# A two-layer graph kernel: statistics of a weight part on ScalarE, and node tiles transposed by DMA

## The chip, the cores and the metric

The kernel runs on one core of a Trainium2 chip. The metric is the device time of one execution in microseconds, the median of several runs. Before the change it is 2240.1 us (three runs, 2240.02 to 2240.91).

## The reference

Two layers work on 3327 nodes with 1024 features each. The first normalises the nodes, quantises them to 4 bits, multiplies them with a quantised 1024 x 1024 weight and sums over the neighbours; the second is graph attention with 8 heads and a small dense network behind it. The change lies in the first product, so only this part matters here:

```python
h = jnp.maximum(_layernorm(x, axis=-1), 0.0)
mean = jnp.mean(weight)
std = jnp.std(weight, ddof=1)
weight_q = _weight_quant((weight - mean) / std, wgt_alpha, 3)
xq = _act_quant(h, act_alpha, 4)
support = jnp.matmul(xq / act_delta, weight_q / wgt_delta) * act_delta * wgt_delta
support_q = _act_quant(jax.nn.relu(support), act_alpha2, 4)
output = jnp.matmul(adj / adj_scaling_factor, support_q / support_delta)
```

The mean and the deviation of the weight go over the whole matrix, so nothing of it can be rounded before all of it has been read.

## The kernel before

The nodes are padded to 26 tiles of 128 rows (T = 26), and the features make 8 blocks of 128 (KF = 8). The work runs in stages: the first computes the quantised support of every tile, `s_int`; the second multiplies it with the adjacency, split into a high and a low part (lines 170 to 179 and 680), and prepares the attention; a third does the attention and a last one the dense layers. This text is about the first stage, lines 194 to 569.

**The weight.** SP issues the two halves of node tile 0, then the eight parts of w, each 128 x 1024 numbers, and then the node tiles 1 to 5. The statistics of a part are made in one of two ways. On VectorE they are two BN_STATS of 512 columns (line 364). On ScalarE (`measure_on_scalar`, lines 248 to 258) they are a pass that sums the part, two small scalings, and a second pass that sums the squares of the deviations; each pass is an ACTIVATE and a read of the accumulator. Parts 0 and 3 go to ScalarE (`BY_ACT`, line 352), the other six to VectorE. One BN_AGGR (line 410) joins all of it, two tiny matmuls with a constant matrix (lines 412 and 419) join the partitions, and then the weight is rounded and clamped in 16 pieces, on ScalarE, VectorE and GpSimd.

**A node tile** goes through these steps. The names in brackets are those of the written order.

- Its rows are loaded on SP in pairs (`load_pair`, line 128), into three buffers of two tiles each. A pair is loaded when ScalarE has read the pair three before it.
- Two BN_STATS and a BN_AGGR on VectorE give mean and variance (stats, mv; lines 234 and 241).
- The norm of a pair of tiles (norm, lines 260 to 287) is a chain of eight tiny operations. Its square root is on ScalarE, the reciprocals are on VectorE, and the rest is on VectorE in the written order and on GpSimd in the loop.
- ScalarE normalises the tile, applies the relu and writes bytes (bytes, line 293). VectorE clips these to 15 and writes bf16 (clip, line 301).
- The tile is transposed into `xqt`, of which there are four buffers. Either a DMA transpose on SP does it, issued in the same step as the clip (line 305), or TensorE does it with eight matmuls into PSUM (turn, line 311) and a copy on ScalarE (turned, line 314). `by_tensor` (line 295) chooses: TensorE takes tiles 0, 1, 2, 3, 4, 6, 9, 12, 15, 18, 21 and 24.
- Sixteen matmuls of 512 columns make the product (product, line 321). ScalarE rescales the result and writes bytes (sum, line 336), and VectorE clips them into `s_int` (support, line 339).

**The order.** Every compute instruction of this stage is pinned to program order on its engine. Up to the product of tile 7 the order is written out by hand as a list of steps, `ORDER` (lines 479 to 509). From tile 8 on a loop makes it (lines 543 to 567): in round t it measures tile t + 6, makes the sum and the support of t - 1, the bytes and the clip of t + 3, and the product of t, between whose halves it transposes tile t + 2 where that is TensorE's. In even rounds it also issues the loads of tiles t + 8 and t + 9, ahead of the transpose of t + 3. SP's queue is in order as well. In round 24 the first adjacency load is issued there (line 170).

Of the kernel before, what the change touches and what calls it, by code (L numbers as in the profile page):

```python
# [8 lines left out]
F32 = mybir.dt.float32  # L9
# [11 lines left out]
P = 128  # L21
N = 3327
T = (N + P - 1) // P
# [3 lines left out]
KF = F // P  # L27
# [33 lines left out]
def two_layer_kernel(  # L61
# [101 lines left out]
    with tc.tile_pool(name="at", bufs=2, reuse_waits="tile") as atp:  # L163
# [35 lines left out]
        with tc.tile_pool(name="s1", bufs=2, reuse_waits="tile") as s1, tc.tile_pool(  # L199
            name="s1_mm", bufs=3, space=PSUM, reuse_waits="tile"  # L200
        ) as mm_ps, tc.tile_pool(name="s1_tp", bufs=2, space=PSUM, reuse_waits="tile") as tp_ps:
            w_int = s1.tile([P, KF, F], BF16, name="w_int", bufs=1)
            w_stats = s1.tile([P, 2 + 4 * (KF - 2), 3], F32, name="w_stats", bufs=1)

            def pin(ins):
                tc.keep_in_program_order(ins)
# [17 lines left out]
            def load_pair(t0):  # L224
                part = load(t0)
                for q in range(GT):
                    part(q)
# [15 lines left out]
            def measure(t):  # L243
                for c in range(FC):
                    half_stats(t, c)
                aggregate(t)

            def measure_on_scalar(mean, squares, src, name):

                junk = s1.tile([P, F], BF16, tag="xq", name="junk", bufs=3)  # L250
                total, nmean = (s1.tile([P, 1], F32, name=name + c, bufs=1) for c in "tm")
                pin(nc.scalar.activation(junk, src, AF.Copy, accum_out=total))
                pin(nc.scalar.activation(nmean, total, AF.Copy, scale=-1.0 / F))
                pin(nc.scalar.activation(mean, total, AF.Copy, scale=1.0 / F))
                yield
                junk = s1.tile([P, F], BF16, tag="xq", name="junk", bufs=3)
                pin(nc.scalar.activation(junk, src, AF.Square, bias=nmean, accum_out=squares))
                yield

            def normaliser(p, engine=nc.gpsimd):  # L260

                v, s, r, q, nb = (
                    small.tile([P, GT], F32, tag=f"l0{c}", name=f"l0{c}") for c in "vsrqb"
                )
                mv = mvs.pop(p)

                def own(ins):
                    if engine is nc.vector:
                        pin(ins)

                own(engine.tensor_scalar(v, mv[:, :, 1], EPS, None, ALU.add))
                yield
                pin(nc.scalar.activation(s, v, AF.Sqrt))
                yield
                pin(nc.vector.reciprocal(r, s))
                yield
                own(engine.tensor_tensor(q, v, r, ALU.mult))
                own(engine.tensor_tensor(q, q, s, ALU.add))
                yield
                pin(nc.vector.reciprocal(r, q))  # L280
                yield
                own(engine.tensor_scalar(r, r, to_q, -1.0, ALU.mult, ALU.mult))
                own(engine.tensor_tensor(nb, mv[:, :, 0], r, ALU.mult))
                own(engine.tensor_scalar(r, r, -1.0, None, ALU.mult))
                for i in range(GT):
                    ready[GT * p + i] = r[:, i : i + 1], nb[:, i : i + 1]
                yield


            def to_bytes(t):  # L290
                rs, nb = ready.pop(t)
                xbs[t] = s1.tile([P, F], U8, name="xb")
                pin(nc.scalar.activation(xbs[t], rows.pop(t), AF.Relu, bias=nb, scale=rs))

            def by_tensor(t):
                return t % 3 == 0 or t in (1, 2, 4)

            def quantise(t, engine=nc.vector):

                xq = xqs[t] = s1.tile([P, F], BF16, name="xq", bufs=3)  # L300
                pin(engine.tensor_scalar(xq, xbs.pop(t), QA, None, ALU.min))

                xqts[t] = s1.tile([P, KF, P], BF16, name="xqt", bufs=4)
                if not by_tensor(t):
                    nc.sync.dma_start_transpose(xqts[t], xqs.pop(t))

            def transpose(t):
                tps[t] = tp_ps.tile([P, KF, P], BF16, name="tp")
                xq = xqs.pop(t)
                for k in range(KF):  # L310
                    pin(nc.tensor.transpose(tps[t][:, k, :], xq[:, k * P : (k + 1) * P], ident_b))

            def transposed(t):
                pin(nc.scalar.copy(xqts[t], tps.pop(t)))
# [19 lines left out]
            def support_bytes(t):  # L334
                sbs[t] = s1.tile([P, F], U8, tag="sb", name="sb", bufs=3)
                pin(nc.scalar.activation(sbs[t], mms.pop(t), AF.Relu, scale=to_s))

            def support(t, engine=nc.vector):
                pin(engine.tensor_scalar(s_int[t], sbs.pop(t), QA, None, ALU.min))
# [9 lines left out]
                loads[q // GT](q % GT)  # L349


            BY_ACT = (0, 3)
            for i in range(len(BY_ACT)):
                nc.gpsimd.memset(w_stats[:, i, 0:1], float(F))
            by_act = [
                measure_on_scalar(w_stats[:, i, 1:2], w_stats[:, i, 2:3], w[:, k], f"w{k}")
                for i, k in enumerate(BY_ACT)
            ]

            def weight_statistics(k):  # L360
                at = len(BY_ACT) + 4 * (k - sum(k > b for b in BY_ACT))
                for c in range(FC):
                    d = w_stats[:, at + 2 * c : at + 2 * c + 2].rearrange("p n s -> p (n s)")
                    pin(nc.vector.bn_stats(d, w[:, k, c * 512 : (c + 1) * 512]))
# [34 lines left out]
            to_s = const.tile([P, 1], F32, name="to_s")  # L399
            nc.gpsimd.tensor_tensor(to_s, act_delta, wgt_delta, ALU.mult)  # L400
            nc.gpsimd.tensor_scalar(to_s, to_s, r_aa2, QA, ALU.mult, ALU.mult)
            for k in (2, 4, 5, 6, 7):
                weight_statistics(k)
                if k == 2:
                    for _ in range(2):
                        next(by_act[1])
                    transposed(0)

            w_mv = small.tile([P, 2], F32, name="w_mv")
            pin(nc.vector.bn_aggr(w_mv, w_stats.rearrange("p n s -> p (n s)")))  # L410
# [61 lines left out]
            def bytes_of(t):  # L472
# [27 lines left out]
                norm_4 product_5_0_5_7 norm_4 product_5_1_0_0 norm_4 product_5_1_1_1 turn_6 norm_4 norm_4  # L500
                product_5_1_2_2 turned_6 support_1 product_5_1_3_5 stats_10_0 product_5_1_6_6 bytes_8
                product_5_1_7_7 product_6_0_0_0 stats_11_0 product_6_0_1_3 support_2 product_6_0_4_4 sum_4
                product_6_0_5_7 clip_8 product_6_1_0_1 sum_5 product_6_1_2_2 stats_10_1 product_6_1_3_5
                stats_11_1 product_6_1_6_6 bytes_9 product_6_1_7_7 product_7_0_0_0 mv_10 product_7_0_1_1
                mv_11 product_7_0_2_2 norm_5 product_7_0_3_3 support_3 product_7_0_4_4 norm_5
                product_7_0_5_6 norm_5 sum_6 product_7_0_7_7 norm_5 product_7_1_0_1 norm_5 product_7_1_2_2
                norm_5 product_7_1_3_4 clip_9 bytes_10 product_7_1_5_7 support_4 turn_9 turned_9 clip_10
                stats_12_0 stats_13_0 stats_12_1 stats_13_1 mv_12 mv_13 support_5 support_6
            """.split()
            V = nc.vector  # L510
            supp = ExitStack()
# [31 lines left out]
            for t in range(8, T):  # L543
                if t == T - 2:
                    part = next(columns)
                pair = t // 2 + 2
                steps = iter(())
                if t % GT == 0 and pair < T // GT:
                    steps = normaliser(pair)
                for _ in range(4):  # L550
                    next(steps, None)
                if t + 6 < T:
                    measure(t + 6)
                for _ in steps:
                    pass
                support_bytes(t - 1)
                support(t - 1)
                if t + 3 < T:
                    to_bytes(t + 3)
                    if t % GT == 0 and t + 8 < T:  # L560
                        load_pair(t + 8)
                    quantise(t + 3)
                products(t, 0)
                if t + 2 < T and by_tensor(t + 2):
                    transpose(t + 2)
                    transposed(t + 2)
                products(t, 1)
            support_bytes(T - 1)
            support(T - 1)
# [2 lines left out]
        with tc.tile_pool(name="wh", bufs=1, reuse_waits="tile") as whp, tc.tile_pool(  # L572
            name="s2", bufs=2, reuse_waits="tile"
        ) as s2, tc.tile_pool(name="mm", bufs=2, space=PSUM, reuse_waits="tile") as mm_ps, tc.tile_pool(
            name="s2_wh", bufs=2, space=PSUM, reuse_waits="tile"
        ) as wh_ps, tc.tile_pool(name="s2_sp", bufs=1, space=PSUM, reuse_waits="tile") as sp_ps, tc.tile_pool(
            name="s2_last", bufs=1, space=PSUM, reuse_waits="tile"
# [90 lines left out]
            for t in range(T):  # L668
# [3 lines left out]
                for js in PARTS:  # L672
                    hi, lo = part
                    part = next(columns, None)
# [54 lines left out]
    with tc.tile_pool(name="mf0", bufs=1, reuse_waits="tile") as mf0, tc.tile_pool(  # L729
        name="srow0", bufs=1, reuse_waits="tile"  # L730
    ) as srow0, tc.tile_pool(name="sel", bufs=4, reuse_waits="tile") as selp, tc.tile_pool(
        name="srow1", bufs=1, reuse_waits="tile"
    ) as srow1, tc.tile_pool(name="mf1", bufs=1, reuse_waits="tile") as mf1, tc.tile_pool(
        name="md", bufs=2, reuse_waits="tile"
    ) as mdp, tc.tile_pool(name="f1", bufs=1, reuse_waits="tile") as f1p, tc.tile_pool(
        name="s3", bufs=1, reuse_waits="tile"
    ) as s3, tc.tile_pool(
        name="s3_acc", bufs=7, space=PSUM, reuse_waits="tile"
# [147 lines left out]
        for i, (c, g, e, si) in enumerate(attends):  # L886
# [82 lines left out]
            for j in range(T):  # L969
                n = i * T + j  # L970
                k, m = divmod(n - 20, 2 * T)
# [43 lines left out]
    with tc.tile_pool(name="s4", bufs=2, reuse_waits="tile") as s4, tc.tile_pool(  # L1015
        name="s4_ps", bufs=4, space=PSUM, reuse_waits="tile"
# [103 lines left out]
```

## Time and profile before

| | |
|---|---|
| median of three runs | 2240.1 us |
| the profiled execution, its time | 2241.67 us |
| its span, first to last instruction | 2239.9 us |
| TensorE busy in the span | 2190.0 us |
| first weight product of a tile (line 321) | 24.74 us |
| first matmul of the second stage (line 680) | 128.41 us |
| mean granted clock of TensorE | 0.998 |

The profiled execution is one execution of the program, and all times in it count from its first instruction. A row of the timeline gives start, length, engine, line and operation, and, in brackets, how long the engine was idle before it and what ended the wait. Rows of the same kind that follow each other are merged. [...] The landing of a DMA is counted from its issue.

### The profile page before, as it was taken

How to read it: one execution, taken by the hardware profiler on the slowest of the kernel's cores; microseconds unless marked ns; L12 is line 12 of the kernel's file. 1: busy time of each engine (PE TensorE's matmuls, PEld its weight loads, DVE VectorE, ACT ScalarE, POOL GpSimd, SP SyncE). 2: the span in 40 equal slices, each digit the busy share in tenths (PEclk: the TensorE clock that was granted, in tenths of full speed). 3: DMA queues.
4: the chain of work that ended last, by engine and by line, in shares of the span. 5: the costliest groups of instructions: out<-in, count | busy, mean ns of one | idle time of the engine just before them, and what ended most of it. 6: DMA issues, size and time to landing. Idle time of an engine off the chain costs nothing.

```text
span 2239.9 us, 31268 instructions
## 1 busy us (share of the span) xinstructions
PE 2190.0 (98%) x12470; PEld 1747.2 (78%) x12480; DVE 1536.8 (69%) x1996; ACT 1114.9 (50%) x1685; POOL 180.4 (8%) x269
## 2 busy tenths in 40 slices
PE   5999999999999999899999999999999999999998
PEld 2477777766677777699999999999999999744444
DVE  8745555554455545588999999999999999822211
ACT  6734444444454444357566556565555655531120
POOL 2301101110111101000000000000000000000000
PEclk9999999999999999999999999999999999999999
DMA  6665566555665556934242341654242432383311
GB/s 216 161 196 158 157 182 183 170 168 146 183 181 171 162 158 189 310 128 148 83 139 88 93 131 33 225 175 151 86 148 83 138 89 77 100 208 104 113 56 56
DMA packets 241203, 321.68 MB, mean 144 GB/s; under 512 B 104021, under 2 KB 184869, under 8 KB 241057
## 3 DMA queue, kind: packets, MB, share of 16 engines
q1 hardware_dynamic: 220504, 246.50, 36.8%
q0 software_dynamic: 20544, 73.18, 10.4%
q8 instruction: 98, 1.61, 0.3%
q14 instruction: 49, 0.39, 0.1%
q10 hardware_dynamic: 8, 0.00, 0.0%
HBM read 209.25 MB, written 86.79 MB: 132 GB/s over the span
## 4 chain that ended last, share of the span: by engine, by line
PE 53%; ACT 1%; DVE 0%; DMA 0%; issue 0%; DVEq 0%
PE acc L993 27%; PE mps L786 13%; PE o L1064 8%; PE h_ps L1027 4%; ACT enct L1049 0%; PE h_ps L949 0%; DMA weights<-in_w1t 0%; ACT h L1034 0%; DVE sel L984 0%; DVE nodes L1060 0%; ACT su L830 0%; DVE su L827 0%; DVE yo L1074 0%; ACT rest L957 0%; DVEq L1117 0%
## 5 line engine op out<-in xcount | busy, mean ns | idle before, releaser
L984 DVE SCALAR_TENSOR_TENSOR sel<-srow,ndst,mask 128x896 fp32r<-128x896 f32 (+1 forms) x832 | 864.8, 1081 | 52.3 <-PE acc L993 47.2
L786 PE MATMUL mps<-dw,mf 128*128 128x260 f32 x2704 | 452.4, 283 | 0.1
L680 PE MATMUL mm<-s_int,hi 128*128 128x512 f32 x1352 | 427.2, 397 | 0.0
L680 PE MATMUL mm<-s_int,lo 128*128 128x512 f32 x1352 | 419.1, 391 | 0.0
L993 PE MATMUL acc<-f_even,sel 128*128 128x260 f32 x2704 | 399.6, 285 | 6.7 <-issue 5.0
L993 PE MATMUL acc<-f_odd,sel 128*128 128x260 f32 x2704 | 393.8, 286 | 1.0 <-ACT xs L1008 1.0
L785 ACT CAST mf<-mask 128x1664 fp32r<-128x1664 uint8 x208 | 331.4, 1594 | 113.0 <-PE mps L786 94.9
L786 PEld LDWEIGHTS mps<-dw,mf 128*128 128x128 f32 x2704 | 377.2, 188 | 0.5 <-ACT part L790 0.3
L993 PEld LDWEIGHTS acc<-f_even,sel 128*128 128x128 f32 x2704 | 356.8, 189 | 11.7 <-issue 5.9
L993 PEld LDWEIGHTS acc<-f_odd,sel 128*128 128x128 f32 x2704 | 352.5, 188 | 8.4 <-issue 3.4
L680 PEld LDWEIGHTS mm<-s_int,hi 128*128 128x128 f32 x1352 | 253.9, 188 | 63.6 <-issue 12.0
L680 PEld LDWEIGHTS mm<-s_int,lo 128*128 128x128 f32 x1352 | 252.0, 188 | 51.4
L179 DVE TENSOR_SCALAR mk<-at 128x896 uint8<-128x896 f32 (+1 forms) x104 | 62.0, 598 | 227.1 <-DMA at<-in_adj_t 226.8
L614 PE MATMUL whm<-whead,ht 128*128 128x512 f32 x416 | 184.4, 596 | 7.2 <-ACT ht L591 7.0
L1064 PE MATMUL o<-weights,h 128*128 128x512 f32 x416 | 179.9, 592 | 0.0
L1064 PEld LDWEIGHTS o<-weights,h 128*128 128x128 f32 x416 | 79.0, 190 | 99.3 <-issue 98.3
L614 PEld LDWEIGHTS whm<-whead,ht 128*128 128x128 f32 x416 | 77.6, 190 | 101.0 <-issue 87.1
L174 ACT CAST hi<-at 128x896 fp32r<-128x896 f32 x104 | 92.4, 889 | 125.6 <-PE mm L680 85.2
L790 ACT COPY part<-mps 128x260 f32<-128x260 f32 x104 | 39.3, 378 | 193.8 <-PE mps L786 193.8
L178 DVE TENSOR_TENSOR lo<-at,hi 128x896 fp32r<-128x896 f32 x104 | 106.0, 1020 | 42.8 <-ACT hi L174 42.6
L855 POOL DMA_DIRECT2D enc_d<-eh x64 | 57.5, 903 | 935.6 <-ACT eh L853 876.0
L1034 ACT ACTIVATE h<-h_ps,rest 128x512 f32<-128x512 f32 (+1 forms) x54 | 35.1, 653 | 195.0 <-PE h_ps L1027 195.0
(162 smaller groups left out, 1676.9 us busy)
## 6 DMA issues: line engine op xcount, KB each, us to landing
feat_d<-fw POOLq DMA_DIRECT2D x26, 1040.0 KB, 5.4
f_even<-feat_d SPq DMA_DIRECT2D x7, 3380.0 KB, 13.3
f_odd<-feat_d SPq DMA_DIRECT2D x7, 3380.0 KB, 13.2
at<-in_adj_t SPq DMA_DIRECT2D x52, 448.0 KB, 3.8
at<-in_adj_t SPq DMA_DIRECT2D x52, 384.0 KB, 3.2
mask<-mask_d SPq DMA_DIRECT2D x39, 416.0 KB, 6.5
dw<-dsum_d SPq DMA_DIRECT2D x16, 910.0 KB, 8.9
dsum_d<-dw POOLq DMA_DIRECT2D x26, 520.0 KB, 6.4
```

What stands on the lines that cost most here:

```text
L174: ins = nc.scalar.copy(hi, at)
L178: nc.vector.tensor_tensor(lo, at, hi.bitcast(F32), ALU.subtract)
L179: ins = nc.vector.tensor_scalar(mk[:, r], at, 0.0, None, ALU.is_gt)
L614: ins = nc.tensor.matmul(whm, ht[:, k, :], whead[:, k, :], start=(k == 0), stop=(k == KF - 1))
L680: nc.tensor.matmul(mm[:, c * 512 : (c + 1) * 512], which[:, q, :], s_int[j][:, c * 512 : (c + 1) * 512], start=(j == 0 and which is hi), s ...
L785: nc.scalar.copy(mf, mask[:, j : j + TH, :])
L786: nc.tensor.matmul(ps, mf[:, j % TH, :], dw[:, j, :], start=(j == 0), stop=(j == T - 1))
L855: nc.gpsimd.dma_start(enc_d[q, sub[0] * P : (sub[-1] + 1) * P, h * HD : (h + 1) * HD].rearrange("(b p) d -> p b d", p=P), eh[:, q].rearran ...
L984: nc.vector.scalar_tensor_tensor(sel[:, :nb], srow[:, :nb], ndst[:, j, h : h + 1], mask[:, :, j, :], ALU.is_gt, ALU.mult,)
L993: nc.tensor.matmul(accs[b], sel[:, b, :], f[:, j, :], start=(j == 0), stop=(j == T - 1))
L1027: nc.tensor.matmul(ps[:, :cols], wt[:, k, m * P : (m + 1) * P], xt[:, k, :cols], start=(k == 0), stop=(k == k_n - 1),)
L1064: nc.tensor.matmul(ps[:, c * 512 : (c + 1) * 512], h3[:, k, q * P : (q + 1) * P], w4[:, k, c * 512 : (c + 1) * 512], start=(k == 0), stop= ...
```

## The change

It has three parts. Part 6 of the weight gets its statistics on ScalarE, as parts 0 and 3 do, and the copy of tile 0's transpose comes behind it on ScalarE. TensorE keeps the transposes of tiles 0, 1, 2, 3, 4 and 6; all tiles from the eighth on, and 5 and 7 as before, go through the DMA transpose. And the hand-written order changes from the product of tile 6 on: bytes and clip of tile 9 come earlier, sum 5 and the norm of pair 5 later in relation to the products, and clip 10 stands among the statistics of tiles 12 and 13 instead of before them.

```diff
-            w_stats = s1.tile([P, 2 + 4 * (KF - 2), 3], F32, name="w_stats", bufs=1)
+            w_stats = s1.tile([P, 3 + 4 * (KF - 3), 3], F32, name="w_stats", bufs=1)
...
             def by_tensor(t):
-                return t % 3 == 0 or t in (1, 2, 4)
+                return t in (0, 1, 2, 3, 4, 6)
...
-            BY_ACT = (0, 3)
+            BY_ACT = (0, 3, 6)
...
-            for k in (2, 4, 5, 6, 7):
+            for k in (2, 4, 5, 7):
                 weight_statistics(k)
-                if k == 2:
-                    for _ in range(2):
-                        next(by_act[1])
-                    transposed(0)
+            for part in by_act[1:]:
+                for _ in range(2):
+                    next(part)
+            transposed(0)
...
-                product_6_0_5_7 clip_8 product_6_1_0_1 sum_5 product_6_1_2_2 stats_10_1 product_6_1_3_5
-                stats_11_1 product_6_1_6_6 bytes_9 product_6_1_7_7 product_7_0_0_0 mv_10 product_7_0_1_1
-                mv_11 product_7_0_2_2 norm_5 product_7_0_3_3 support_3 product_7_0_4_4 norm_5
-                product_7_0_5_6 norm_5 sum_6 product_7_0_7_7 norm_5 product_7_1_0_1 norm_5 product_7_1_2_2
-                norm_5 product_7_1_3_4 clip_9 bytes_10 product_7_1_5_7 support_4 turn_9 turned_9 clip_10
-                stats_12_0 stats_13_0 stats_12_1 stats_13_1 mv_12 mv_13 support_5 support_6
+                product_6_0_5_7 clip_8 product_6_1_0_1 bytes_9 product_6_1_2_2 stats_10_1 product_6_1_3_5
+                stats_11_1 product_6_1_6_7 sum_5 product_7_0_0_0 clip_9 product_7_0_1_3 mv_10
+                product_7_0_4_4 mv_11 product_7_0_5_5 norm_5 product_7_0_6_6 support_3 norm_5
+                product_7_0_7_7 product_7_1_0_1 norm_5 product_7_1_2_2 sum_6 norm_5 product_7_1_3_4 norm_5
+                product_7_1_5_5 norm_5 product_7_1_6_7 stats_12_0 bytes_10 stats_13_0 stats_12_1 clip_10
+                stats_13_1 support_4 mv_12 mv_13 support_5 support_6
...
                 products(t, 0)
-                if t + 2 < T and by_tensor(t + 2):
-                    transpose(t + 2)
-                    transposed(t + 2)
                 products(t, 1)
```

## The prediction

> **What bounds the kernel now.** I read three views, in this order: the page's busy table, the order of time on each engine in the first 130 us, and the sums over chosen stretches.
>
> ```profile
> PE 2190.0 (98%) x12470; PEld 1747.2 (78%) x12480; DVE 1536.8 (69%) x1996; ACT 1114.9 (50%) x1685; POOL 180.4 (8%) x269
> ```
>
> TensorE is busy for all but 50 us, so from about 128 us on the kernel is a queue of matmuls: whatever time the first stage ends earlier or later, the end should move by the same amount. The change touches only the first stage. What TensorE does there (start, length, idle time before and its cause in brackets):
>
> ```profile
> 61.33 0.61 PE L311 MATMUL tp<-ident_b,xq 128*128 128x128 bf16 x8
> 61.78 8.80 PE L321 MATMUL mm<-w_int,xqt 128*128 128x512 bf16 x39
> 71.84 0.62 PE L311 MATMUL tp<-ident_b,xq 128*128 128x128 bf16 x8 [1.26 <-DVE xq L301]
> 72.30 1.89 PE L321 MATMUL mm<-w_int,xqt 128*128 128x512 bf16 x8
> 75.00 8.81 PE L321 MATMUL mm<-w_int,xqt 128*128 128x512 bf16 x39 [0.82 <-DMA xqt<-xq]
> 83.65 0.61 PE L311 MATMUL tp<-ident_b,xq 128*128 128x128 bf16 x8
> 84.09 10.52 PE L321 MATMUL mm<-w_int,xqt 128*128 128x512 bf16 x47
> 94.45 0.61 PE L311 MATMUL tp<-ident_b,xq 128*128 128x128 bf16 x8
> ```
>
> Two regimes are to be seen. From 75.00 to the end of the stage at 128.4 TensorE never waits. Before 75 it does, and the wait is for data of tile 11. I count tiles back from the end: 16 matmuls of a tile take 3.45 us (10.81 us from transpose to transpose, less 0.44, over three tiles), so 75.00 is the start of tile 11, 71.84 is tile 12's transpose, and 61.33, 83.65 and 94.45 are those of 9, 15 and 18. What tile 11 hangs on is this chain, in order of time:
>
> ```profile
> 64.51 0.33 DVE L241 BATCH_NORM_AGGREGATE mv<-stats 128x2 f32<-128x12 f32 x2
> 65.00 1.04 POOL L271 TENSOR_SCALAR l0v<-mv 128x2 f32<-128x2 f32 x1 [30.65 <-DVE mv L241]
> 66.07 0.20 ACT L273 ACTIVATE l0s<-l0v 128x2 f32<-128x2 f32 x1 [3.08 <-POOL l0v L271]
> 67.17 1.23 ACT L293 ACTIVATE xb<-xs,l0b,l0r 128x1024 uint8<-128x1024 f32 x1
> 68.43 0.81 SPq L128 DMA_DIRECT2D xs<-in_x  x2
> 69.40 1.24 SPq L305 DMA_TRANSPOSE xqt<-xq  x1
> ```
>
> ScalarE waits 3.08 us for the variance of pair 6 (tiles 12 and 13), and the bytes of tile 11 stand behind it. They free a buffer, two x loads go out on SP ahead of tile 11's transpose, and this lands 5.6 us after its issue, at 75.0.
>
> The weight's statistics, at the start:
>
> ```profile
> 11.48 1.06 ACT L252 ACTIVATE junk<-w 128x1024 bf16<-128x1024 f32 x1
> 14.00 0.19 ACT L257 ACTIVATION_READ_ACCUMULATOR junk<-w,w3m 128x1 f32 x1
> 12.76 5.13 DVE L364 BATCH_NORM_STATS2 w_stats<-w 128x6 f32<-128x512 f32 x8 [1.18 <-DMA w<-in_w]
> 17.99 0.51 DVE L410 BATCH_NORM_AGGREGATE w_mv<-w_stats 128x2 f32<-128x78 f32 x1
> ```
>
> SP issues the first x loads at 7.63, 8.91, 10.19, 11.47 and 12.75, each when a part of w has landed: one part of 512 KB every 1.28 us. Parts 5, 6 and 7 are then due at 14.03, 15.31 and 16.59 (worked out). VectorE needs 1.28 us for a part, so its eight statistics run exactly behind the arrivals.
>
> Last, the granted clock:
>
> ```profile
> 31.20:34.60 3.40, 1.71 (x5) 0.48 (x5) 3.33 (x8) 2.64 (x4) 2.83 (x5) 1.00 0.00 0
> 34.60:38.00 3.40, 3.18 (x14) 1.69 (x14) 3.37 (x9) 2.62 (x3) 0.00 (x0) 0.50 0.52 166
> 932.30:935.70 3.40, 0.00 (x0) 0.02 (x1) 3.31 (x5) 3.38 (x4) 2.24 (x3) 1.00 1.09 354
> 935.70:942.50 6.80, 6.31 (x26) 5.72 (x27) 6.80 (x11) 1.16 (x3) 0.00 (x0) 0.50 1.05 398
> ```
>
> The columns are the busy times of PE, PEld, DVE, ACT and POOL, then the clock. Twice a stretch of 3.4 us with TensorE half busy or idle is followed by half the clock for 3.4 or 6.8 us.
>
> **What the Trainium skill says.** "TensorE: Matmul & The Clock Gate", Part 1, says that the array runs at half its clock after an idle window of about 3.4 us, in windows that do not start with the kernel; the four lines above agree (3.4 us, 0.50). "DMA: Bandwidth & Descriptors", Issuing engines are not separate DMA queues, says that all DMAs share 16 engines and interleave: a transpose landed 3.0 us after its issue at 106.8 with nothing else moving, and 5.6 us behind two loads. "GPSIMD Engine Reference", in the table of the engine's properties, says that GpSimd shares its SBUF interfaces with VectorE: POOL's 128x2 operation took 1.04 us beside two VectorE rounds of s_int, against 0.22 us elsewhere.
>
> **The change, part by part.**
>
> *Weight part 6 to ScalarE.* VectorE loses two statistics (1.28 us), but part 7 still lands at 16.59, so its end stays at 17.89. ScalarE took 2.71 us from the start on part 3 (11.48) to its end (14.19); from 15.31 that is 18.02. The aggregate then starts about 0.1 us later, at 18.08, and reads 69 numbers in place of 78 (0.51 us x 9/78 = 0.06 less). Sum: +0.03, taken as 0; bounds -0.06 (part 6 lands early) and +0.3 (ScalarE's two passes slow beside the loads). Behind them on ScalarE waits the copy of tile 0's transpose, 1.0 us, now to 19.0; TensorE reads it at 19.9. The cover is 0.9 us, and if it were gone the loss would be what exceeds it. One memset more on GpSimd is at 1.5 us, in idle time.
>
> *The written order, tiles 6 to 11.* The bytes of tile 9 move ahead of sum 5: 56.4 to 57.6 in place of 57.4 to 58.6. Its clip then comes at 57.7, ahead of the aggregates of 10 and 11. The norm of pair 5 starts at 59.35 in place of 58.74 and ends at 60.8; the bytes of tile 10 end at 62.1, and its clip at 63.2 (before 62.2). Statistics 12 and 13 go around this clip, and support 4 ahead of their aggregates: these end at 64.6 in place of 64.84. So the chain above starts 0.2 us earlier, and nothing else of it changes. Tile 11 lands at 74.8. Bounds for this step: 0.5 each way.
>
> *TensorE's transposes of 9 and 12 go.* This saves 2 x 0.44 and the wait of 1.26, but tile 11 is no earlier for it. Tile 8 starts at 61.33, 9 at 64.8, 10 at 68.25 and ends at 71.7. The new transposes: tile 9 is issued at 58.6 behind two loads, lands near 63.7 and is wanted at 64.8; tile 10 is issued at 63.4, lands near 66.7 and is wanted at 68.25; tile 12 follows 11 and lands near 76.5, wanted at 78.2. So both waits and two transposes become one wait of about 3.0 us for tile 11: no gain.
>
> *The other four (15, 18, 21, 24).* TensorE is the bound there, so 4 x 0.44 = 1.76 us go, with four copies of 1.0 us on ScalarE, which had room. Queue: a pair of tiles asks the DMA engines for two loads (1.28 us each at the rate of w) and two transposes (the one issued at 106.8 kept them busy for 0.76 of the 1.8 us from 107.6, which is 1.4 us): 5.4 of TensorE's 6.9 us. A transpose is issued about 3.4 us after its tile's slot opens (tile 17: slot 85.85, issue 89.26), lands 3.0 to 5.6 later and is wanted 10.35 after: 1.4 us to spare at the worst. On SP a pair takes 2 x 1.24 + 0.81 = 3.3 us.
>
> *The clock.* A wait of 3.0 us fills most of a 3.4 us window. The stretch at 31.2 dropped the clock with 1.71 us of 3.40 busy; the one from 70.45 to 75.00, with 2.47 of 4.55, did not. I take it that half the clock for one window follows, over tile 11's matmuls: 1.7 us lost. Bounds: 0 and 3.4.
>
> *The handover.* The first adjacency load was issued at 119.27 and its two halves were ready at 125.2, 3.2 us ahead of TensorE. It comes behind tile 25's transpose, whose issue moves with TensorE, so the cover stays near 2.8 us.
>
> Sum: 0 - 0.2 - 1.76 + 1.7 = -0.3 us. The profiled execution has a span of 2239.9 and a time of 2241.67, so 1.8 lie around it; it would be 2241.4. The median of the runs, 2240.1, lies 1.6 below that execution, and I take the difference from it: 2239.8.
>
> **The rivals.**
> 1. *No drop of the clock.* The wait falls across two windows, or is shorter than 3 us. For it: 2.1 us of idle time in 70 to 75 did no harm. Then -2.0: 2238.1.
> 2. *The DMA queue becomes the bound (slower).* If a transpose among loads holds the engines for 3.0 us, its whole latency alone, a pair needs 2.56 + 6.0 = 8.6 us against 6.9. The loads run until tile 25's, which is seven pairs: 7 x 1.65 = 11.5, less the 2.0 saved: 2249.6. It decides from 2.2 us for a transpose on, is a loss against before from 2.3, and over 0.2% from 2.65. For it: 5.6 us landings. Against: the 1.4 us of activity of one alone.
> 3. *Tile 11 is freed too*, so that both waits and all six transposes go: 2.1 + 6 x 0.44 = 4.7: 2235.4. Against: its chain names VectorE, GpSimd and ScalarE, and none of these lost work in it.
> 4. The change does do what it says: six transposes move to SP, by the order of the instructions; no rival there.
>
> **How the numbers follow.** Forecast 0.45, rival 1 0.33, rival 2 0.10, rival 3 0.05; 0.07 is for a second stage whose DMA waits (seven for ht, 7.0 us in all) fall otherwise by 1 to 3 us. A measurement of this kernel can tell about 0.2%, 4.5 us, from no change. Faster takes most of rival 3: 0.04. Slower takes rival 2: 0.10. Same: 0.86. The range holds the forecast and rival 1 with their bounds and half of the rest: 2237.2 to 2241.8.
>
> **What would show it.** Right: the aggregate of w_mv at about 18.1, released by ScalarE; one wait of TensorE of about 3 us ahead of tile 11 at 74.8, released by the DMA of xqt; clock 0.50 for 3.4 us right after; then matmuls without a gap, and the first L680 near 128. Wrong: waits on xqt in every pair from tile 13 on, or tile 11 started before 74.

## The result, and the profile after

Ten runs of the changed kernel have a median of 2246.3 us (2243.9 to 2247.5), ten of the kernel before beside them 2240.8 (2239.9 to 2242.6). The ratio is 1.0022, interval 1.0015 to 1.0030: a small loss of 5.5 us, outside the predicted range. The profiled execution took 2245.84 us with a span of 2244.1; that is 4.2 us more than the span before.

The first stage came out much as the prediction has it. This is the order of time on TensorE in the changed kernel; the columns are start, length, engine, line and operation, and the bracket gives the wait before it. Matmul rows overlap: 102.80 and 24.35 make 127.15, and the next row starts at 126.80.

```profile
53.02 18.73 PE L321 MATMUL mm<-w_int,xqt 128*128 128x512 bf16 x84
74.45 27.80 PE L321 MATMUL mm<-w_int,xqt 128*128 128x512 bf16 x125 [2.71 <-DMA xqt<-xq]
102.80 24.35 PE L321 MATMUL mm<-w_int,xqt 128*128 128x512 bf16 x110 [0.55 <-DMA xqt<-xq]
126.80 0.81 PE L677 MATMUL mm<-s_int,hi 128*128 128x512 f32 x2
```

One wait ahead of tile 11, one small wait at 102.80, and the second stage begins at 126.80 instead of 128.41: 1.6 us earlier. On the engines that measure the weight, the same view shows VectorE waiting for part 7 and ScalarE ending part 6 last:

```profile
16.58 1.29 DVE L364 BATCH_NORM_STATS2 w_stats<-w 128x6 f32<-128x512 f32 x2 [1.26 <-DMA w<-in_w]
...
17.77 0.19 ACT L257 ACTIVATION_READ_ACCUMULATOR junk<-w,w6m 128x1 f32 x1
17.87 0.99 ACT L314 COPY xqt<-tp 128x1024 bf16<-128x1024 bf16 x1
18.06 0.47 DVE L410 BATCH_NORM_AGGREGATE w_mv<-w_stats 128x2 f32<-128x69 f32 x1 [0.19 <-ACT junk L257]
```

So the loss arises behind the stage that was changed. The two profiles part like this:

| from the span's start, us | before | after | difference |
|---|---|---|---|
| tile 11's product starts | 75.00 | 74.45 | -0.55 |
| second stage, first matmul | 128.41 | 126.80 | -1.61 |
| third stage, first `acc` matmul | 935.71 | 938.80 | +3.09 |
| end of the span | 2239.9 | 2244.1 | +4.2 |

The second stage took 807.3 us before and 812.0 after. Nothing of its code was changed; only its line numbers are three lower. What TensorE waits for is a sum over the whole span: line, what it waited for, total us, times, longest. Before:

```profile
PE whm L614 <- ACT ht L591: 7.0, 7, 1.4
```

and after:

```profile
PE whm L611 <- ACT ht L588: 11.4, 10, 2.6
...
PE mm L321 <- DMA xqt<-xq: 3.5, 3, 2.7
```

These are the waits for `ht` that the prediction left at the edge of its account, seven before and ten after: 4.4 us more of them, which is nearly all of the stage's 4.7. The remaining 1.1 us at the end lies behind it. At the border to the third stage the clock is at half for 10.2 us instead of 6.8, and there is one new wait of 0.7 us for a load of `dw`; other small differences take some of that back.

**The path to `ht`.** In the second stage each of 25 node tiles y is turned for the attention's product: ScalarE splits its 32-bit words into halves (`yh`), a DMA transpose on SP writes `yht`, ScalarE puts the words together again in one copy of 2.5 us (`ht`), and the products `whm` read it. Tile 5 shows both cases, at nearly the same time in both kernels. Before:

```profile
316.03 3.42 SPq L589 DMA_TRANSPOSE yht<-yh  x1
...
321.48 2.51 ACT L591 COPY ht<-yht 128x2048 uint16<-128x2048 uint16 x1 [3.00 <-DMA yht<-yh]
...
324.24 3.17 PE L614 MATMUL whm<-whead,ht 128*128 128x512 f32 x7
```

After:

```profile
316.35 4.99 SPq L586 DMA_TRANSPOSE yht<-yh  x1
...
323.40 2.48 ACT L588 COPY ht<-yht 128x2048 uint16<-128x2048 uint16 x1 [4.70 <-DMA yht<-yh]
...
325.93 1.55 PE L611 MATMUL whm<-whead,ht 128*128 128x512 f32 x3 [1.31 <-ACT ht L588]
```

Before, the copy ends at 323.99 and the product starts 0.25 us later without a wait: that quarter of a microsecond is all the slack of the path in this tile. After, the transpose needs 7.05 us from its issue to the copy instead of 5.45, and TensorE stops for 1.31.

What differs between the two is in the view of the DMA queues over the 7.2 us from the issue on. The rows are packets, MB and the share of the 16 engines; the first row is the rate in 40 slices of 0.18 us; the last one ends in the landing time. Before, from 316.0:

```profile
GB/s 364 364 387 296 296 97 86 68 68 85 222 427 375 398 353 270 279 168 104 276 293 292 292 284 293 292 181 124 68 0 68 182 250 341 478 410 364 404 378 364
...
q1 hardware_dynamic: 2395, 1.55, 85.5%
q0 software_dynamic: 93, 0.32, 14.7%
...
yht<-yh SPq DMA_TRANSPOSE x1, 5.4
```

After, from 316.3:

```profile
GB/s 364 432 364 250 313 68 103 51 85 171 256 375 344 367 285 313 280 122 74 18 6 17 0 17 17 0 13 17 174 293 287 292 289 293 287 433 189 114 68 23
...
q1 hardware_dynamic: 2249, 1.02, 95.4%
q0 software_dynamic: 91, 0.31, 14.1%
q8 instruction: 1, 0.02, 0.8%
...
yht<-yh SPq DMA_TRANSPOSE x1, 7.0
```

There is one packet more, on a queue of kind "instruction". It starts at 319.3 and takes 0.89 us on one DMA engine. In the slices 19 to 27 (counted from 0: 319.7 to 321.3), where the transpose before ran at some 290 GB/s, the rate falls to under 20; the burst comes after it, and the landing is 1.6 us later.

**What that queue is.** The page of the changed kernel counts it over the whole span:

```profile
PE 2188.2 (98%) x12423; PEld 1744.6 (78%) x12432; DVE 1535.3 (68%) x1994; ACT 1112.1 (50%) x1685; POOL 180.7 (8%) x270
...
q8 instruction: 97, 1.59, 0.3%
```

97 packets of 16 KB for 12423 + 12432 instructions of TensorE is one packet for 256 instructions; before it is 98 for 24950. The Trainium skill, "Advanced Engine Details and Errata", section ISA Cache, says that a line of the instruction cache is 16 KB, 256 instructions; these counts agree. A second count agrees: in all ten profiles, each packet of the second stage begins 142 to 186 instructions into a block of 256 (two for each weight load, counted from TensorE's first), however many instructions the experiments below put in front. So queue 8 is taken for TensorE's instruction fetch.

In the second stage it comes about once in a tile (24 packets before and 25 after, for 26 tiles). A tile has 242 instructions there (104 matmuls of L677, 16 of L611 and one small one, each with its load), so the packet comes 14 instructions later from tile to tile, 1 to 2 us, and meets the same place again after some 18 tiles. A run of tiles thus has a fetch up to 5.5 us behind the issue of the transpose (called struck here), and the tiles after it have none. Before, these are tiles 10 to 14 (0.4, 1.8, 1.5, 4.2 and 4.9 us behind the issue); after, tiles 3 to 7 and 21 to 24. The waits ahead of these tiles sum to 4.0 us before and 10.6 after.

Not every wait is one of these. Before, tiles 7, 9 and 24 wait without such a fetch (0.85, 1.01 and 1.17); after, tiles 9 and 12 do (0.66 and 0.16). In tiles 9 and 24 of both kernels queue 0 moves 0.6 to 0.7 MB within 7.2 us of the issue and in every other tile 0.4 or less, which may be their cause and was not tried. The 2.62 us ahead of tile 24 after the change are thus a fetch on top of a wait that the other kernels have there too (1.2 to 1.3 in before and after + 96).

The change takes away six transposes of eight matmuls, each with its weight load: 96 instructions of TensorE. All later fetches come 96 instructions later in the program, which at 14 instructions a tile is about seven tiles.

### The profile page after: what moved, and what is told of

It reads as the page before. It is cut to its first block, busy times and chain, and to the rows that moved or that the text cites. A ratio compares the mean times of both kernels' runs of the same rounds, so it can differ in the third digit from the quotient of the medians.

```text
span 2244.1 us, 31186 instructions
## 1 busy us (share of the span) xinstructions
PE 2188.2 (98%) x12423; PEld 1744.6 (78%) x12432; DVE 1535.3 (68%) x1994; ACT 1112.1 (50%) x1685; POOL 180.7 (8%) x270
## 4 chain that ended last, share of the span: by engine, by line
PE 53%; ACT 1%; DVE 0%; DMA 0%; issue 0%; SPq 0%; DVEq 0%
PE acc L990 27%; PE mps L783 13%; PE o L1061 8%; PE h_ps L1024 4%; ACT enct L1046 0%; PE h_ps L946 0%; DMA weights<-in_w1t 0%; DVE sel L981 0%; ACT h L1031 0%; DVE nodes L1057 0%; SPq L931 0%; ACT su L827 0%; DVE su L824 0%; DVE yo L1071 0%; ACT rest L954 0%
## 5 line engine op out<-in xcount | busy, mean ns | idle before, releaser
L677 PE MATMUL mm<-s_int,hi 128*128 128x512 f32 x1352 | 427.1, 397 | 0.0
L677 PE MATMUL mm<-s_int,lo 128*128 128x512 f32 x1352 | 419.3, 391 | 0.0
L677 PEld LDWEIGHTS mm<-s_int,hi 128*128 128x128 f32 x1352 | 253.9, 188 | 63.8 <-issue 12.0
L677 PEld LDWEIGHTS mm<-s_int,lo 128*128 128x128 f32 x1352 | 252.0, 188 | 51.3
L611 PE MATMUL whm<-whead,ht 128*128 128x512 f32 x416 | 184.5, 596 | 11.4 <-ACT ht L588 11.4
L611 PEld LDWEIGHTS whm<-whead,ht 128*128 128x128 f32 x416 | 77.4, 190 | 105.7 <-issue 87.1
```

The source lines that it names most:

```text
L611: ins = nc.tensor.matmul(whm, ht[:, k, :], whead[:, k, :], start=(k == 0), stop=(k == KF - 1))
L677: nc.tensor.matmul(mm[:, c * 512 : (c + 1) * 512], which[:, q, :], s_int[j][:, c * 512 : (c + 1) * 512], start=(j == 0 and which is hi), s ...
```

## The experiments

**The theory:** the 96 missing instructions move the phase of the fetch against the transposes of the second stage, and this costs the loss. **Rival A:** the six transposes that went to SP do it, since they shift which DMA engines and descriptors later transfers get. **Rival B:** the earlier start of the second stage does it, by moving the tiles against transfers that keep their time. In the first two experiments and in two later ones, idle matmuls of one column are put behind the first broadcast (line 376), where TensorE waits anyway; they write an unused column of a bank and change nothing that is computed. Each is two instructions, a load and a product.

**The 96 instructions given back**

```diff
+            for _ in range(48):
+                pin(nc.tensor.matmul(row_ps[:1, 512:513], ident_b[:, :1], ident_b[:, :1], start=True, stop=True))
```

> The changed kernel with 96 instructions more on TensorE (48 one-column matmuls and their weight loads, into an unused bank, while TensorE waits at the start). Fetch theory: the six transposes that went were 96 instructions, so TensorE's program again meets the second stage at the place in its 16 KB fetch blocks where the kernel before meets it; the fetches fall on the yht transposes of about tiles 9 to 14 as before, the waits of whm for ht return from 11.4 to about 7 us, and only the 1.6 us won in the first stage are left: 2239 to 2240 us. Rival, the six DMAs more on SP (their lanes, or the transposes themselves) disturb the second stage: nothing of that is undone, 2246 us. Rival, the second stage starts 1.6 us earlier and meets other transfers: also 2246 us.

Measured: 2240.6 us (2238.0 to 2245.9, 13 runs) against 2241.0 of the kernel before (23 runs), ratio 0.9996 (0.9988 to 1.0004). The loss is gone with the order and all DMAs of the change in place, so rival A falls; the second stage began at 126.65, so rival B falls too. In the sum of waits:

```profile
PE whm L613 <- ACT ht L590: 6.8, 6, 1.4
...
PE mm L321 <- DMA xqt<-xq: 2.9, 3, 2.5
```

The struck tiles are again 10 to 14. The first stage's gain of 1.6 us was expected to remain; the interval (-2.7 to +0.9 us) is too wide to show it.

**The kernel before, with instructions added.** 160 more is the phase of 96 fewer, since a packet holds 256.

```diff
+            for _ in range(80):
+                pin(nc.tensor.matmul(row_ps[:1, 512:513], ident_b[:, :1], ident_b[:, :1], start=True, stop=True))
```

> The kernel before with 160 instructions more on TensorE at the start (80 one-column matmuls and their loads), that is 256 less 96: its place in the fetch blocks becomes that of the changed kernel, with nothing of the change made. Fetch theory: the fetches fall on the yht transposes of about tiles 3 to 7 and 21 to 24, and the time goes up by the loss without the 1.6 us gain: 2246 to 2248 us. Both rivals: nothing of the change is in it, 2240.8 us.

Measured: 2247.3 us (8 runs), ratio 1.0027 (1.0017 to 1.0037). The kernel before, with no part of the change, loses what the change lost. Its waits are nearly the changed kernel's, and its struck tiles are 3 to 7 and 22 to 24 (the fetch of tile 21 comes 0.9 us ahead of its transpose, and in the changed kernel together with it; neither waits):

```profile
PE whm L616 <- ACT ht L593: 10.9, 9, 2.4
```

**A whole packet added to the changed kernel** (128 idle matmuls, 256 instructions), to see whether it is the phase or the presence of idle matmuls that helps.

```diff
+            for _ in range(128):
+                pin(nc.tensor.matmul(row_ps[:1, 512:513], ident_b[:, :1], ident_b[:, :1], start=True, stop=True))
```

> The changed kernel with 256 instructions more on TensorE at the start (128 one-column matmuls and their loads), one whole fetch block. Control for the padding itself. Fetch theory: the place in the blocks is that of the changed kernel, so 2246 us. If padding as such helps, by warming the clock or by moving the start, about 2240 us.

Measured: 2247.5 us (8 runs), ratio 1.0027 (1.0017 to 1.0037), 10.5 us of waits in 8 tiles, struck tiles 3 to 7 and 22 to 24. The loss stays: a full packet leaves the phase where it was.

**A third phase** (96 idle matmuls, 192 instructions).

```diff
+            for _ in range(96):
+                pin(nc.tensor.matmul(row_ps[:1, 512:513], ident_b[:, :1], ident_b[:, :1], start=True, stop=True))
```

> The changed kernel with 192 instructions more on TensorE, one look for the place of the fetches. 96 moved the tiles that are struck from 3 to 7 to 10 to 14, so seven tiles later; 192 should strike 17 to 21, and one period of about 18 tiles earlier, 0 to 3. Any rival: the long waits for ht stay at tiles 3 to 7 and 22 to 24.

Measured, in one run: 2243.6 us, 8.6 us of waits in 10 tiles, of which 5.5 us lie ahead of six struck ones. The struck tiles are those that had been computed, 0 to 3 and 17 to 21; the time of a single run proves little.

These kernels beside each other, and three of those that follow, by their profiles (the stage from its first matmul to the first `acc` matmul):

| kernel | second stage, us | waits for `ht`, us | struck tiles |
|---|---|---|---|
| before | 807.3 | 7.0 | 10-14 |
| after | 812.0 | 11.4 | 3-7, 21-24 |
| after + 96 | 807.0 | 6.8 | 10-14 |
| before + 160 | 813.9 | 10.9 | 3-7, 22-24 |
| after + 256 | 814.1 | 10.5 | 3-7, 22-24 |
| after + 192 | 809.1 | 8.6 | 0-3, 17-21 |
| after, `ht` in halves | 799.7 | 1.7 | 3-7, 21-24 |
| before, `ht` in halves | 798.3 | 0.3 | 10-14 |
| after, heads later | 844.6 | 36.3 | 23 tiles wait, struck or not |

Two rows are longer than their waits explain, before + 160 and after + 256. In both the wait of tile 24 (2.4 and 2.6 us) was followed by a lower clock. In the sums over stretches of after + 256 (busy us of PE, PEld, DVE, ACT and POOL, then the clock, the DMA share and GB/s):

```profile
922.10:925.50 3.40, 3.37 (x4) 1.51 (x5) 0.00 (x0) 0.00 (x0) 0.00 (x0) 0.50 1.05 380
925.50:928.90 3.40, 3.40 (x6) 1.41 (x5) 0.00 (x0) 0.00 (x0) 0.00 (x0) 0.59 1.01 342
```

The same 16 matmuls took 10.20 us there and 7.13 in the profile after, where the wait of 2.62 had no such effect. So the loss of one execution depends on this too; when it comes is taken up below, with the clock.

**Slack by moving the next step.** `heads`, which holds the products behind `ht`, is called two node blocks (eight matmuls) later, to give the transpose more time.

```diff
-                    if js is PARTS[-1] and before is not None:
-                        heads(*before)
                     for q, j in enumerate(js):
                         for which in (hi, lo):
...
+                        if js is PARTS[-1] and before is not None and q == 2:
+                            heads(*before)
```

> The changed kernel, with the head products of a tile issued after two of the six node blocks of the last part in place of ahead of them: eight matmuls of the adjacency product, 1.8 us, stand between. Fetch theory: the wait for ht, 2.6 us at most and 1.4 in most tiles, is covered by these matmuls; of the 11.4 us at least 9 go: 2235 to 2238 us. If the waits are not what costs the time, 2246 us.

Measured: 2274.0 us (4 runs), ratio 1.0146 (1.0130 to 1.0161): a miss. The transpose's own view shows why; after first, then this kernel:

```profile
L586 SPq DMA_TRANSPOSE yht<-yh x25: 3351/3572/5760, 160.2 to 909.1; - x25
...
DMA to landing us min/median/max: 5.3/5.6/7.2
```

```profile
L586 SPq DMA_TRANSPOSE yht<-yh x25: 3567/5956/7517, 161.3 to 943.7; - x25
...
DMA to landing us min/median/max: 7.1/7.7/8.9
```

Most transposes are now some 2 us later, and TensorE waits for 36.3 us in 23 tiles. `heads` also ends in writes of 1040 and 520 KB to memory (`feat_d`, `dsum_d`), and these moved with it: ahead of tile 5 the second is now issued at 319.77, 4.3 us before the transpose at 324.04, where in the changed kernel it was 6.0 us before it (310.40 and 316.35). So transposes can be late without a fetch. That the writes are the cause is read from the trace and was not tried by itself.

**Slack by splitting the copy.** `ht` is written in two copies of half the blocks, and the first products need only the first half. This changes neither transposes nor fetches, only how late a transpose may land.

```diff
-                nc.scalar.copy(
-                    halves_of_words(ht.rearrange("p k i -> p (k i)")),
-                    yht.rearrange("p (two k) i -> p two (k i)", two=2),
-                )
+                y2 = yht.rearrange("p (two k) i -> p two k i", two=2)
+                for k in (slice(0, KF // 2), slice(KF // 2, KF)):
+                    nc.scalar.copy(
+                        halves_of_words(ht[:, k].rearrange("p k i -> p (k i)")),
+                        y2[:, :, k].rearrange("p two k i -> p two (k i)"),
+                    )
```

In the changed kernel:

> The changed kernel with ScalarE's copy of yht into ht made in two halves (feature blocks 0 to 3, then 4 to 7), so that the head products can start after the first. If the waits for ht are what the change lost, each shrinks by half a copy, about 1.2 us of 2.5: of the 11.4 us in ten tiles some 2 are left, and the time falls by 9 us, to 2236 to 2238 us, below both kernels. If the fetch does its harm elsewhere, little changes and it stays near 2246 us.

In the kernel before:

> The kernel before with the same two halves. Its seven waits of 7.0 us shrink to about 0.5: 2234 to 2236 us. Against the changed kernel with the same edit this shows what the first stage wins, with the second stage's waits nearly out of it: the changed one is faster by 0 to 2 us.

Measured: 2232.1 us (5 runs, ratio 0.9962, 0.9949 to 0.9976) in the changed kernel and 2231.9 (5 runs, ratio 0.9966, 0.9954 to 0.9979) in the kernel before. The ratios are against the kernel before. Both are faster than either kernel without the split, by more than was expected, and of the 0 to 2 us that the changed one was to be ahead nothing is seen. Tile 5 of the changed kernel with the split:

```profile
313.85 4.89 SPq L586 DMA_TRANSPOSE yht<-yh  x1
...
320.73 2.54 ACT L590 COPY ht<-yht 128x1024 uint16<-128x1024 uint16 x2 [4.33 <-DMA yht<-yh]
...
322.16 7.11 PE L613 MATMUL whm<-whead,ht 128*128 128x512 f32 x16
```

The transpose is as late as before (6.88 us from issue to copy), but the product starts 1.43 us behind the start of the copies and waits for nothing. The gain is larger than the waits removed: in the kernel before, 6.7 us of waits went, and the stage became 9.0 shorter. A part of this may be that the first `whm` row overlaps the row before it by 0.16 us where it need not wait: with the split nine or ten tiles more have this overlap, some 1.5 us by this estimate. The rest was not settled.

**The weight part alone**, put into the kernel before: part 6 on ScalarE and the copy of tile 0 behind it, nothing else.

```diff
-            BY_ACT = (0, 3)
+            BY_ACT = (0, 3, 6)
```

> The kernel before with the weight's part of the change alone (part 6 on ScalarE, the copy of tile 0's transpose behind it). TensorE's program is as before, so the fetch theory gives no loss in the second stage; the aggregate of w_mv starts at 18.06 and ends as before: 2240.8 us. If this part carries the loss, 2246 us.

Measured: 2240.4 us (13 runs), ratio 1.0000 (0.9992 to 1.0008), 7.0 us of waits for `ht`. This part does nothing to the time, as predicted; no instruction of TensorE changes with it.

## Why the prediction was wrong

- **Weight part 6: right.** The aggregate was put at 18.08, released by ScalarE; it came at 18.06. Alone, this part gave 1.0000.
- **The written order, and transposes 9 and 12: right.** One wait of about 3.0 us ahead of tile 11 at 74.8 was predicted; it was 2.71 us, and the tile started at 74.45.
- **Transposes 15, 18, 21 and 24: the mechanism right, the size a little off.** From tile 11 to the second stage it was 53.41 us before and 52.35 after, of which 0.55 is a wait for a DMA transpose (tile 19's) that the prediction had ruled out with "1.4 us to spare at the worst". It was issued at 96.89, 5.4 us before its product's turn and not the 7.0 that the prediction's figures give, and took 5.9. So 1.06 us came instead of 1.76; 52.04 with 96 instructions given back, with a wait of 0.19.
- **The clock behind that wait: right in some executions.** Of six profiles with this wait, two kept the clock and four lost one window. With the drop it was 53.4 to 53.7 us from tile 11 to the second stage, against 53.41 before: the drop eats the four transposes. The forecast and rival 1 were both seen. The prediction laid its windows where the waits were. But in each of the ten profiles all changes of the granted clock from the first drop on lie on a grid of 3.413 us, and its offset differs from profile to profile. Here are the grid's windows in the profile after (clock kept), then in the changed kernel with `ht` in halves (clock lost):

```profile
69.10:72.51 3.41, 2.64 (x13) 0.98 (x10) 2.96 (x8) 3.05 (x4) 1.09 (x4) 1.00 1.00 305
72.51:75.92 3.41, 1.47 (x7) 0.70 (x8) 3.34 (x9) 2.28 (x3) 1.56 (x3) 1.00 1.15 243
75.92:79.33 3.41, 3.41 (x18) 1.55 (x16) 2.87 (x9) 1.91 (x4) 0.95 (x3) 1.00 1.06 283
```

```profile
70.23:73.64 3.41, 0.73 (x4) 0.31 (x4) 3.38 (x8) 2.77 (x4) 1.80 (x5) 1.00 1.18 234
73.64:77.05 3.41, 3.41 (x10) 1.21 (x8) 2.95 (x8) 1.10 (x2) 0.94 (x3) 0.50 1.10 321
```

  A wait of 2.7 us is split by a border of the grid in the first (0.77 and 1.94 us) and falls into one window in the second. In the four profiles with the drop, TensorE was idle for 2.1 to 2.7 us of the window ahead of it; in the two without, for 1.94 at most. "TensorE: Matmul & The Clock Gate", Part 1, says that the window is free-running and about 3.4 us long, which agrees. It speaks of an idle window; here one with 0.7 to 1.3 us of work in it was enough, and the measurement decides.
- **The end follows the first stage: wrong, and this is the step that failed.** It said that from about 128 us on the kernel "is a queue of matmuls: whatever time the first stage ends earlier or later, the end should move by the same amount". The first stage ended 1.6 us earlier and the end came 4.2 later. The second stage is a queue of matmuls with a path beside it that has some tenths of a microsecond of slack in each tile, and where fetches strike this path is set by how many instructions TensorE has fetched since the start. The change removed 96, which moved the strikes from five tiles to nine; the waits grew from 7.0 to 11.4 us. Giving 96 back took the loss away, and adding 160 to the kernel before made it.
- **The case that named it was mis-sized.** The last 0.07 of the chances was for these seven waits, "otherwise by 1 to 3 us". They gave 4.4 in the profile. Against the medians it is 5.5, and up to 7 in executions that keep the first stage's 1.6 us; the lower clock behind tile 24's wait, which two other profiles of this phase show, may be the rest.
- **Rival 2, the slower one, was not it.** Waits on `xqt` were 3.5 us in three places, not in every pair.

## What to carry to other kernels

Before saying that a later stage only moves with an earlier one, list the waits of that stage and the slack on each path beside its bound: where a path has tenths of a microsecond, a change elsewhere that alters the number of instructions can make or lose microseconds there. Here the waits were 7, 8.6 or about 11 us by that number alone. A small loss or gain that appears in code which was not touched is tested by putting idle instructions in or taking them out; if it moves with their number alone, it belongs to the phase and not to the change. The cure is slack, not phase: two copies in place of one on the tight path brought both kernels to 8 us below the kernel before, more than the change was expected to bring.

## What was not expected of the hardware

- TensorE's instruction fetch runs on the DMA engines beside the data: 97 packets of 16 KB, 0.3% of their time. In the ten profiles nine packets in ten take 0.9 to 1.3 us, the longest 2.3. Leaving out the kernel with `heads` later, and tile 24, 45 transposes of `yht` had a fetch 1.4 to 5.0 us behind their issue: 44 of them took 6.4 to 7.5 us to the copy, one 5.3. With a fetch 0.2 to 0.7 us behind it took 5.7 to 6.0, and without one 5.1 to 6.2 (tiles 9, 12 and 24 aside). "DMA: Bandwidth & Descriptors", section Issuing engines are not separate DMA queues, says that all DMAs share 16 engines and interleave; that one packet of 0.9 us goes with a delay of 1.6, as in tile 5, is more than that says. How it does so was not tried; the trace shows only that the transpose's packets pause and resume.
- Whether a wait of TensorE of 2.4 to 2.8 us halved the clock went with how much of it fell into one window of the 3.41 us grid. At tile 24 the drop followed windows with 1.96 and 2.08 us idle (after + 256, before + 160) and not one with 1.90 (after). No sharp border is shown: in the kernel with `heads` later a window with 1.84 was followed by the drop, and in the profile after one with 1.94 was not.
